# A relational graph layer on one core: loads in other pieces, bookkeeping moved between the table's steps, more gather buffers and a new written order

## The chip, the cores and the metric

The kernel runs on one core of a Trainium2 chip. The metric is the device time of one execution in microseconds (us), taken as the median of several runs. All data are float32 or int32 in DRAM; the inputs are laid out in other shapes on the host before the launch, and that takes no device time.

## The reference

One layer of a graph network with 625 nodes of width 512, 20,625 edges sorted by their target, and four relations:

```python
h = relu(layernorm(x))
for r in range(4):
    w_r = where(edge_type == r, edge_weight, 0)
    total_msg += (h[src] @ W_rel[r] + b_rel[r]) * w_r[:, None]
agg = segment_sum(total_msg, dst) / maximum(segment_sum(edge_weight, dst), 1)[:, None]
x1  = layer_norm(h + h @ W_self + b_self + agg, ln1_g, ln1_b)
ffn = gelu(x1 @ W_ffn1 + b_ffn1) @ W_ffn2 + b_ffn2          # 512 -> 1024 -> 512
out = x + layer_norm(x1 + ffn, ln2_g, ln2_b)
```

The edges are random, so the message rows have to be fetched by index or summed through a matrix that is built from the indices.

## The kernel before

**Tiles and blocks.** The nodes lie in five blocks of 128 (`NB`), the edges in 162 tiles of 128 (`NT`). As the edges are sorted by target, each tile belongs to one block or to two neighbours: tiles 0 to 30 to block 0, 130 to 161 to block 4, and the rest to blocks 1 to 3 and to the borders between blocks. Blocks 0 and 4 are called outer (`OUTER`), blocks 1 to 3 inner. A table of 4 x 5 = 20 chunks (`NC`) of 128 rows holds h @ W_rel[r] + b_rel[r] for every relation and node block.

**First stage: 20 steps.** The step number is r * NB + i. `table_rows` (L470) multiplies the transposed normalised x of block i with `wr_sb[r]`, four f32 matmuls; VectorE (DVE) scales the sum out of PSUM into `tr` (L483), adds the bias and has it stored to the table in DRAM; the last chunks stay in SBUF too (`kept`). Between these steps the rest of the bookkeeping is issued, each piece at a step that a constant names:

- Edge sums of the outer blocks. For block 0 and the first 15 tiles of block 4 (`LINES`), `line_columns` and `line_sums` work out for every edge the cell of a 128 x 2560 matrix that it adds to, joining the weights of equal cells, and GpSimd (POOL) scatters the weights to the cleared `cells` in DRAM with one indirect DMA a tile, 46 in all (`scatter`, L750; columns become ready at the steps of `COLUMNS_AT`, two scatters are issued in each of the steps 0 to 2 and all that are ready in later ones). The remaining 17 tiles of block 4 are "banked": they become one-hot matrices on DVE (`node_hots` L648, `weighted_hots` L666, the first of them at `HOTS_AT`) that are multiplied on TensorE (PE) in `outer_sum` (L680).
- `outer_columns` and `edge_columns` (at `COLUMNS_OF_EDGES_AT`) turn the loaded edge columns into float and into table rows `row_i`; `group_columns` and `degree_columns` follow at `GROUPS_AT`.
- `degree_hots` (L844, at `DEGREE_HOTS_AT` and, for the outer tiles, `OUTER_HOTS_AT`), `degree_sums` and `degree_end` (`DEGREES_AT`) make the sums of the edge weights and the counts of edges for each node; `spread_rows` (`SPREAD_AT`, L970 to L977) spreads them, `counts` among them, and `first_edges` (L906, `FIRST_AT`) multiplies the counts on PE to find where each node's edges begin. `load_first_edges` then has POOL gather `x_edges`, three indirect DMAs.
- The layer norm of x in other blocks: `centre_x` and `spread_x` on ScalarE (ACT), `rsqrt_pow` (L399) on POOL, at `NORM_AT` and `ROOT_AT`. Two norms are made ahead of the first step by `pre_norm`.
- `set_limits` (L534): 72 small ACT writes, half at step 4 and half at step 6 (`LIMITS_AT`), that `count_outside` (L542) uses to see whether an edge lies outside the range its tile was planned for. In that case a general loop runs at the end; with these inputs it doesn't.
- `tensor_add` of bias rows on x (L1235, `ADDS_AT`) and of the identity on `ws_sb` (L1245, `SELF_AT`).

**Loads.** They are issued by hand at the start, in this order: the two column halves of x block 0 (one on ACT's queue, one on that of SyncE, SP), quarters 0 and 1 of `wr_sb[0]`, x block 1, quarter 2, the line of edges of block 0 (`load_line`, 128 overlapping windows of one row), quarter 3, x block 2, bias rows, x blocks 3 and 4, the clearing of the cells, the edge columns, and later ones.

**Second stage.** It is a list of 700 operations (`Plan.op`), each with its engine, what it comes after and which buffers it takes and gives back. `Plan.written` issues them in the order that the constant `ORDER` writes out; all engines follow that one list, each its own part of it. If `ORDER` is empty, `Plan.times` makes an order from the costs; the constants `CELLS`, `FIRSTS`, `LAND` and `LATE` are read only there. The operations are:

- for the inner blocks and borders, in the order (3,4), (0,1), (1), (1,2), (2,3), (3), (2): POOL gathers table rows by `row_i` into one of ten buffers `ms` (L1312, 99 tiles, and three rows from `gather_first`). Three tiles make a group with common targets: ACT scales the first row (`first_row`), DVE adds the other two (`row_added`, L1348), then ACT and DVE split the sum into a high and a low fp32r part (`high`, `low`) and PE multiplies both with the one-hot `oh` (`edge_sum`, L1373), or, where the group stands whole (`parted`, `WHOLE`: every second group of the last sum, and its last three), one f32 product. In the last sum PE runs five small matmuls (`spin`, L1400) ahead of each of its last four (`SPINS`) units.
- for the outer blocks, 20 `chunk_sum` products each (L1489) of the matrix `sums_w`, loaded back from `cells`, with the table's chunks.
- for every block: `self_part` (L508), the first norm, `turn` and its copies (L1552), `ups` (L1058) with gelu, `downs` (L1078), the final norm (L1088 to L1103) and the stores. Block 2 comes last. Its final norm takes its root by `root_steps`: a square root on ACT, whose function table an extra `root_of` activation loads ahead, and a division step on DVE, for which `g2_bc` is scaled beforehand. The other blocks take their root by `rsqrt_steps` or, where `ROOTS` says POOL, by a power on POOL.

Of the kernel before, what the change touches and what calls it, by code (L numbers as in the profile page):

```python
# [16 lines left out]
P = 128  # L17
EG = 3
# [3 lines left out]
LINES = 999, 15  # L22


class EdgePlan:
# [84 lines left out]
class Plan:  # L110
# [48 lines left out]
    def times(self):  # L159
# [5 lines left out]
        while left:  # L165
# [27 lines left out]
            if not can:  # L193
                times = [e[0] for e in back] + list(free.values())
                times += [max(a.at + d for a, d in o.after) for o in left
                          if o.after and all(a.at is not None for a, _ in o.after)]
                t = min(x for x in times if x > t + 1e-6)
        return order


@with_exitstack
def gnn_layer(ctx, tc, x, edges, edge_line, edge_groups, w_self, w_rel, w_ffn1, w_ffn2, rows_in, bf_in, out, n_edges):

# [73 lines left out]
    def load_x(b0, b1):  # L277
        nc.sync.dma_start(xs[:, b0:b1, :], x[ep.first[b0]:ep.first[b0] + (b1 - b0) * P, :].rearrange("(b p) d -> p b d", p=P))
# [1490 lines left out]
```

## Time and profile before

| | |
|---|---|
| median of 3 runs | 258.41 us (257.94 to 258.63) |
| profiled execution | 257.69 us, span 255.8 us |
| mean granted TensorE clock | 0.992 |
| PE busy | 240.3 us, 94% of the span |
| DVE busy | 196.8 us, 77% |
| POOL busy | 171.5 us, 67% |
| ACT busy | 112.2 us, 44% |
| DMA | 59.44 MB, 232 GB/s over the span |

The span runs from the first to the last recorded instruction; the execution's time has what lies around it as well, here 1.9 us. In the lists of instructions a row gives the start, the length (us), the engine, the line of the program, the operation with output <- input, the shapes, how many instructions were joined, and in brackets how long the engine stood idle before it and what released it ("issue": nothing that the profile shows). A grouped row gives the count, the busy sum, the mean in ns, and the idle time before the group's instructions. A row of a window gives the span, then the busy time and the count for PE, PEld (weight loads of PE), DVE, ACT and POOL, then the granted clock, and the DMA engines' busy share and rate. Busy time of PE is the time that matmuls are in flight, so 94% is no statement on how much of it is needed.

### The profile page before, as it was taken

The page shows a single profiled execution, that of the slowest core. Times are in us where ns is not written, and L with a number is a line of the kernel's source. Part 1 is how long each engine was busy: PE and PEld are TensorE (multiplying, and loading weights), DVE is VectorE, ACT ScalarE, POOL GpSimd, SP SyncE. Part 2 cuts the span into 40 slices and gives each one's busy share as a digit, 9 for nine tenths or more (in the row PEclk, how much of TensorE's full clock was granted, in tenths as well). Part 3 has the DMA queues.
Part 4 walks back from the last instruction along what each step waited for, and adds up shares of the span by engine and source line. Part 5 has one row for each costly group of instructions (what it writes and reads, how often), then busy time and mean ns, then how long its engine had stood idle before and what let it go on. Part 6 is the DMA issues. An engine that isn't in the chain of part 4 may idle for free.

```text
span 255.8 us, 3608 instructions
## 1 busy us (share of the span) xinstructions
PE 240.3 (94%) x1051; PEld 141.9 (55%) x1051; DVE 196.8 (77%) x466; ACT 112.2 (44%) x345; POOL 171.5 (67%) x218
## 2 busy tenths in 40 slices
PE   7899999999969997997999999999999999978992
PEld 6354444444434753544545575666986668536871
DVE  3694699999996329997898889997795897767153
ACT  3378700000610007766147555747666565542620
POOL 5028888988998877877777777777777777701000
PEclk9999999999997999999999999999999999999999
DMA  6999999994361499887999986677777777621021
GB/s 175 345 406 409 377 350 349 331 324 167 83 249 41 110 342 281 302 279 241 304 324 361 376 300 196 188 214 197 214 215 209 204 190 192 214 65 41 3 82 43
DMA packets 23998, 59.44 MB, mean 232 GB/s; under 512 B 4420, under 2 KB 8744, under 8 KB 22823
## 3 DMA queue, kind: packets, MB, share of 16 engines
q0 software_dynamic: 9728, 26.79, 35.0%
q1 hardware_dynamic: 13920, 30.91, 33.7%
q10 hardware_dynamic: 326, 1.48, 1.9%
q8 instruction: 9, 0.15, 0.2%
q14 instruction: 15, 0.11, 0.2%
HBM read 49.99 MB, written 9.17 MB: 231 GB/s over the span
## 4 chain that ended last, share of the span: by engine, by line
PE 35%; DVE 31%; issue 12%; POOL 8%; DMA 8%; ACT 2%; SPq 1%; DVEq 0%; POOLq 0%; ACTq 0%
PE ps L1058 8%; PE acc L1489 7%; PE ps L1078 6%; PE acc L1373 5%; POOL ms L1312 4%; PE ps L508 4%; DVE tr L483 4%; PE ps L470 3%; DVE z L496 3%; POOL cells L750 3%; DMA line<-in_edge_line_dram 3%; DMA ms<-table,row_i 3%; DVE add L1348 3%; DMA x_edges<-in_edge_groups_dram,x_group 2%; DVE same L737 2%
## 5 line engine op out<-in xcount | busy, mean ns | idle before, releaser
L1312 POOL DMA_INDIRECT ms<-table,row_i x99 | 99.6, 1006 | 30.2 <-issue 14.8
L470 PE MATMUL ps<-wr,T 128*128 128x512 f32 (+2 forms) x168 | 72.6, 587 | 0.5 <-DMA wr<-in_L_gnn_W_rel_dram 0.5
L750 POOL DMA_INDIRECT cells<-weight,cell x46 | 52.8, 1148 | 15.5 <-DVE tr L483 8.2
L470 PEld LDWEIGHTS ps<-wr,T 128*128 128x128 f32 x168 | 31.3, 194 | 35.7 <-issue 31.9
L1348 DVE SCALAR_TENSOR_TENSOR add<-ms,wgt_g,add 128x512 f32<-128x512 f32 x55 | 40.5, 749 | 6.4 <-DMA ms<-table,row_i 3.5
L1058 PEld LDWEIGHTS ps<-T,w_sb 128*128 128x128 f32 x320 | 38.5, 192 | 5.4 <-issue 1.7
L1058 PE MATMUL ps<-T,w_sb 128*128 128x128 f32 (+2 forms) x320 | 39.4, 276 | 1.2 <-ACT T L1552 0.8
L1078 PE MATMUL ps<-w_sb,gT 128*128 128x512 f32 (+2 forms) x96 | 36.4, 522 | 0.0
L666 ACT ACTIVATE ohw<-os,w 128x128 fp32r<-128x128 f32 x34 | 10.8, 388 | 48.5 <-DVE os L648 48.5
L1318 ACT ACTIVATE add<-ms,wgt_g 128x512 f32<-128x512 f32 x30 | 20.4, 685 | 20.6 <-DVE el L1326 13.4
L1489 PE MATMUL acc<-tr,sums_w 128*128 128x512 f32 x60 | 29.3, 595 | 0.0
L1078 PEld LDWEIGHTS ps<-w_sb,gT 128*128 128x128 f32 x96 | 16.8, 191 | 13.9 <-issue 11.2
L1326 DVE TENSOR_TENSOR el<-add,eh 128x512 fp32r<-128x512 f32 x25 | 16.9, 685 | 6.1 <-PE acc L1373 3.7
L1322 ACT CAST eh<-add 128x512 fp32r<-128x512 f32 x25 | 14.6, 585 | 15.2 <-DVE add L1348 15.1
L1373 PE MATMUL acc<-eh,oh 128*128 128x512 f32 x34 | 18.0, 544 | 1.9 <-ACT eh L1336 1.4
L508 PE MATMUL ps<-ws_sb,T 128*128 128x512 f32 x40 | 18.7, 593 | 0.0
L1373 PE MATMUL acc<-el,oh 128*128 128x512 f32 x34 | 17.5, 538 | 0.2 <-DVE el L1340 0.2
L1064 ACT ACTIVATE gT<-ps,bf 128x128 f32<-128x128 f32 (+1 forms) x40 | 13.5, 359 | 7.0 <-PE ps L1058 6.7
L483 DVE SCALAR_TENSOR_TENSOR tr<-ps,rx,brel_bc 128x512 f32<-128x512 f32 x15 | 11.2, 745 | 5.6 <-POOL rx L399 5.6
L1489 PEld LDWEIGHTS acc<-tr,sums_w 128*128 128x128 f32 x60 | 10.6, 190 | 7.9 <-issue 6.0
L508 PEld LDWEIGHTS ps<-ws_sb,T 128*128 128x128 f32 x40 | 7.4, 190 | 7.1 <-issue 6.9
L1373 PEld LDWEIGHTS acc<-eh,oh 128*128 128x128 f32 x34 | 6.5, 190 | 7.4 <-issue 3.3
(240 smaller groups left out, 310.8 us busy)
## 6 DMA issues: line engine op xcount, KB each, us to landing
tr<-table SPq DMA_DIRECT2D x11, 512.0 KB, 5.5
w_sb<-in_L_gnn_W_ffn_dram SPq DMA_DIRECT2D x2, 2048.0 KB, 10.5
table<-tr SPq DMA_DIRECT2D x15, 256.0 KB, 5.9
wr<-in_L_gnn_W_rel_dram SPq DMA_DIRECT2D x3, 1024.0 KB, 7.6
cells<-zeros SPq DMA_DIRECT2D x2, 1280.0 KB, 9.2
ms<-table,row_i POOLq DMA_INDIRECT x99, 4.0
rows<-in_rows_dram SPq DMA_DIRECT2D x1, 1280.0 KB, 12.3
sums_w<-cells ACTq DMA_DIRECT2D x1, 1280.0 KB, 8.3
```

The source lines that it names most:

```text
L470: nc.tensor.matmul(p_[:, :h.stop - h.start], hT[i][:, k, :], wr_sb[r][:, k, h], start=(k == 0), stop=(k == KD - 1))
L483: made_row.append(nc.vector.scalar_tensor_tensor(m[:, h], p_[:, :h.stop - h.start], rx[:, i, 1:2], brel_bc[:, r * D + h.start:r * D + h.st ...
L508: nc.tensor.matmul(p[0], hT[i][:, k, :], ws_sb[:, k, :], start=(k == 0), stop=(k == KD - 1))
L750: s = nc.gpsimd.indirect_dma_start(out=cells[i][:, :], out_offset=bass.IndirectOffsetOnAxis(ap=cell[i][:, k:k + 1], axis=0), in_=weight[i] ...
L1058: nc.tensor.matmul(pu[:, low:nn + first], w1_sb[:, k, f * P:(f + 1) * P], x1T_b()[:, k, low:nn + first], start=(k == 0), stop=(k == KD - 1))
L1078: nc.tensor.matmul(po[h][:n, :w], box["gT"][:, f, at], w2_sb[:, f, c], start=(f == 0), stop=(f == KF - 1))
L1312: nc.gpsimd.indirect_dma_start(out=ms[j], out_offset=None, in_=table[:, :], in_offset=bass.IndirectOffsetOnAxis(ap=row_i[:, j:j + 1], axis=0))
L1318: nc.scalar.activation(box["sum"], ms[j], AF.Copy, scale=wgt_g[:, (j - GROUP0) // EG, 0:1])
L1326: nc.vector.tensor_sub(box["low"], box["sum"], box["high"].bitcast(F32))
L1348: nc.vector.scalar_tensor_tensor(to, ms[j], wgt_g[:, k, q:q + 1], box["sum"], op0=ALU.mult, op1=ALU.add)
L1373: nc.tensor.matmul(acc[bs], w.bitcast(F32) if of.dtype == F32 else w, of, start=first, stop=last)
L1489: nc.tensor.matmul(acc[b,], sums_w[b][:, c, :], kept[(b, c) if (b, c) in kept else c], start=first, stop=last)
```

## The change

- **Loads.** x comes in a second layout `x_by_row` (partition, block, column), in which one partition's rows are contiguous; x block 0 is loaded in two halves of the partitions, and its statistics are taken over the whole width at once (`x_stats`). `edge_line` is laid out with one contiguous row for each partition, and the line of block 0 comes in two pieces: three fields, and the weights later, after the bias rows. `wr_sb[0]` comes in two halves in place of four quarters, both ahead of the line.
- **Tiles.** 14 tiles of block 4 are scattered in place of 15, and 18 are banked. One scatter is issued in step 0, three in step 1, four in step 2.
- **Bookkeeping.** `set_limits` takes a slice: 18 of the writes for the lower limits come ahead of the first transposed copies, the rest after them, and the upper limits at step 4. `outer_columns` and `edge_columns` go from step 5 to 2, `group_columns` and `degree_columns` from 6 to 4, `degree_hots` from 9 and 12 to 5 and 6, those of the outer tiles from 15 and 16 to 6 and 8, `degree_end` from 14 to 9, `spread_rows` from 16 to 11, `first_edges` from 17 to 13; the third call of `next_columns` from step 4 to 3. The additions to x go from 15, 17, 18 to 5, 9, 16, the identity from 13 to 15, the pre-made one-hots from 13, 14, 16 to 14, 15, 16. The powers of blocks 3 and 4 are one instruction at step 2. The edge types in float (`typ_f`) have a tile of their own that ends with the first stage.
- **Gather buffers.** When `chunk_sum` has used them, the two `sums_w` matrices (five buffers each) and the five `kept` chunks are appended to `ms`: 25 buffers in place of 10, each given back to the order at the matmul that used it last.
- **Last rows.** `WHOLE` is 5. The last group of the last sum isn't joined: its three tiles are units of one tile each, whose one-hots carry the weights (`edge_hots`), and whose rows go from the gather straight into f32 products. `SPINS` is 6.
- **Roots.** `root_steps`, `root_of` and both scalings of `g2_bc` are gone; block 2's final root is taken by POOL.
- **Order.** `ORDER` is a new list, of 702 operations (PE 222 to 227, DVE 200 to 198, ACT 150 to 148, POOL 104 to 105, SP 19 and 19).

The diff, without the numbers of `ORDER` and without the places that pass `x_by_row` on:

```diff
-LINES = 999, 15
+LINES = 999, 14
...
 ORDER = [
...
 ]
...
     def load_x(b0, b1):
-        nc.sync.dma_start(xs[:, b0:b1, :], x[ep.first[b0]:ep.first[b0] + (b1 - b0) * P, :].rearrange("(b p) d -> p b d", p=P))
+        nc.sync.dma_start(xs[:, b0:b1, :], x_by_row[:, b0:b1, :])
...
-    def load_line(i):
-        at = sum(n * P + 2 * NEAR + 1 for _, _, n in lines[:i])
-        n = lines[i][2]
-        nc.sync.dma_start(line[i], bass.AP(tensor=edge_line.tensor, offset=edge_line.offset + at,
-                                           ap=[[n, P], [edge_line.shape[1], 4], [1, n + 2 * NEAR + 1]]))
+    def load_line(i, f0=0, f1=4):
+        at = sum(4 * (n + 2 * NEAR + 1) for _, _, n in lines[:i])
+        w = lines[i][2] + 2 * NEAR + 1
+        nc.sync.dma_start(line[i][:, f0:f1, :].rearrange("p f w -> p (f w)"), edge_line[:, at + f0 * w:at + f1 * w])
...
-    nc.scalar.dma_start(xs[:, 0, D // 2:], x[:P, D // 2:])
-    nc.sync.dma_start(xs[:, 0, :D // 2], x[:P, :D // 2])
-    load_wr(0, [(0, 1)])
-    load_wr(0, [(1, 2)])
+    nc.scalar.dma_start(xs[P // 2:, 0, :], x_by_row[P // 2:, 0, :])
+    nc.sync.dma_start(xs[:P // 2, 0, :], x_by_row[:P // 2, 0, :])
+    load_wr(0, [(0, 2)])
...
-    load_wr(0, [(2, 3)])
-    load_line(0)
-    load_wr(0, [(3, 4)])
+    load_wr(0, [(2, 4)])
+    load_line(0, 0, 3)
...
+    load_line(0, 3, 4)
...
     def x_stats(i):
-        st = work.tile([P, 2 if i == 0 else 1, 6], F32, tag="bn", name=f"st_x{i}", bufs=HOTS)
-        w = D // st.shape[1]
-        for h in range(st.shape[1]):
-            nc.vector.bn_stats(st[:, h, :], xs[:, i, h * w:(h + 1) * w])
+        st = work.tile([P, 6], F32, tag="bn", name=f"st_x{i}", bufs=HOTS)
+        nc.vector.bn_stats(st, xs[:, i, :])
...
-    fl = const.tile([P, 3, NT], F32, name="fl")
-    src_f, dst_f, typ_f = fl[:, 0, :], fl[:, 1, :], fl[:, 2, :]
+    fl = const.tile([P, 2, NT], F32, name="fl")
+    src_f, dst_f, typ_f = fl[:, 0, :], fl[:, 1, :], early.tile([P, NT], F32, name="typ_f")
...
-    def set_limits(a):
-        j0 = 0
-        for j in range(1, NT + 1):
-            if j == NT or limits[j][a] != limits[j0][a]:
-                nc.scalar.activation(lim[:, a, j0:j], node_row[:, :j - j0], AF.Copy, scale=0.0, bias=float(limits[j0][a]))
-                j0 = j
+    def set_limits(a, of=slice(None)):
+        at = [j for j in range(1, NT) if limits[j][a] != limits[j - 1][a]]
+        for j0, j in [*zip([0, *at], [*at, NT])][of]:
+            nc.scalar.activation(lim[:, a, j0:j], node_row[:, :j - j0], AF.Copy, scale=0.0, bias=float(limits[j0][a]))
...
-        nc.vector.tensor_copy(fl, ed[:, 0:3, :])
-        nc.vector.tensor_scalar(shift, fl[:, 0:2, :], float(ep.gap_at), float(ep.gap), op0=ALU.is_ge, op1=ALU.mult)
-        nc.vector.tensor_add(fl[:, 0:2, :], fl[:, 0:2, :], shift)
-        nc.vector.tensor_copy(node_i, fl[:, 0:2, :])
+        nc.vector.tensor_copy(fl, ed[:, 0:2, :])
+        nc.vector.tensor_copy(typ_f, ed[:, 2, :])
+        nc.vector.tensor_scalar(shift, fl, float(ep.gap_at), float(ep.gap), op0=ALU.is_ge, op1=ALU.mult)
+        nc.vector.tensor_add(fl, fl, shift)
+        nc.vector.tensor_copy(node_i, fl)
...
-    def root_steps(box, first):
-
-        def root():
-            nc.scalar.activation(box["t"][:, 1:2], box["t"][:, 0:1], AF.Sqrt)
-
-        def improve():
-            v, y, a = (box["t"][:, j:j + 1] for j in range(3))
-            nc.vector.reciprocal(y, y)
-            nc.vector.scalar_tensor_tensor(a, y, v, y, op0=ALU.mult, op1=ALU.mult)
-            nc.vector.scalar_tensor_tensor(y, a, 3.0, y, op0=ALU.subtract, op1=ALU.mult)
-
-        return [("root", "ACT", 0.25, root, [first]), ("r3", "DVE", 0.55, improve, ["root", "a"])]
-
     def feed_forward(x1T_b, box, members, name, halves=False, first=False, root="DVE", low=0):
...
-            norm += [] if halves else pow_step(got) if root == "POOL" else rsqrt_steps(got, "mean", root)
+            norm += pow_step(got) if root == "POOL" else rsqrt_steps(got, "mean", root)
...
-            norm += root_steps(got, "mean") if halves else []
...
-    SPINS = 4
+    SPINS = 6
...
-    HOTS_AT, SELF_AT, ADDS_AT = (13, 14, 16), 13, (15, 17, 18)
+    HOTS_AT, SELF_AT, ADDS_AT = (14, 15, 16), 15, (5, 9, 16)
...
-    WHOLE = 3
-    POW, ROOTS = 0.9, (("ACT", "ACT", "POOL", "ACT", "ACT"), ("ACT",) * 5)
-    CELLS, FIRSTS = 1.5, 5.0
+    WHOLE = 5
+    POW, ROOTS = 0.9, (("ACT", "ACT", "POOL", "ACT", "ACT"), ("ACT", "ACT", "POOL", "ACT", "ACT"))
+    CELLS, FIRSTS = 4.0, 0.5
...
-    COLUMNS_AT, LINE_AT, DEGREE_HOTS_AT = (0, 1, 4, 7, 10, 11, 13), 8, (9, 12)
-    COLUMNS_OF_EDGES_AT, GROUPS_AT, LOAD_AT, LIMITS_AT = 5, 6, 15, (4, 6)
-    DEGREES_AT, SPREAD_AT, FIRST_AT, OUTER_HOTS_AT = 14, 16, 17, (15, 16)
-    NORM_AT, ROOT_AT = ((0, 2), (1, 3), (2, 4)), ((1, 2), (2, 3), (3, 4))
+    COLUMNS_AT, LINE_AT, DEGREE_HOTS_AT = (0, 1, 3, 7, 10, 11, 13), 8, (5, 6)
+    COLUMNS_OF_EDGES_AT, GROUPS_AT, LOAD_AT, LIMIT_CUT, LIMITS_AT = 2, 4, 15, 18, 4
+    DEGREES_AT, SPREAD_AT, FIRST_AT, OUTER_HOTS_AT = 9, 11, 13, (6, 8)
+    NORM_AT, ROOT_AT = ((0, 2), (1, 3), (2, 4)), ((1, 2, 3), (2, 3, NB))
...
+        set_limits(0, slice(LIMIT_CUT))
...
+        set_limits(0, slice(LIMIT_CUT, None))
...
-                if step in dict(ROOT_AT):
-                    spread_x(dict(ROOT_AT)[step])
-                    rsqrt_pow(rx[:, dict(ROOT_AT)[step], :])
-                if step in LIMITS_AT:
-                    set_limits(LIMITS_AT.index(step))
+                for _, b0, b1 in (a for a in ROOT_AT if a[0] == step):
+                    for b in range(b0, b1):
+                        spread_x(b)
+                    nc.gpsimd.tensor_tensor(rx[:, b0:b1, 1], rx[:, b0:b1, 0], half.to_broadcast([P, b1 - b0]), op=ALU.pow)
...
-                for _ in range(2 if step < 3 else len(columns)):
+                if step == LIMITS_AT:
+                    set_limits(1)
+                for _ in range((1, 3, 4)[step] if step < 3 else len(columns)):
...
-                nc.vector.tensor_scalar(ohs[0][:, q, :], row, d[:, j_:j_ + 1], wgt[:, j_:j_ + 1],
+                to, w_ = j_, wgt[:, j_:j_ + 1]
+                if GROUP0 <= j_ < GROUP0 + EG * GROUPS:
+                    g_, q_ = divmod(j_ - GROUP0, EG)
+                    to, w_ = j_ - q_ + EG // 2, wgt_g[:, g_, q_:q_ + 1]
+                nc.vector.tensor_scalar(ohs[0][:, q, :], row, d[:, to:to + 1], w_,
...
-            if GROUP0 <= j < GROUP0 + EG * GROUPS and (j - GROUP0) % EG:
+            if GROUP0 <= j < GROUP0 + EG * GROUPS and (j - GROUP0) % EG and (bs != order_of[-1] or j + EG <= tiles[-1]):
...
+    more_rows = {}
+    for b in OUTER:
+        of = sums_w[b].rearrange("p c n -> p (c n)")
+        more_rows[b] = [len(own_buffers["ms"]) + i for i in range(NC * P // D)]
+        own_buffers["ms"] += [of[:, i * D:(i + 1) * D] for i in range(NC * P // D)]
+    for c in range(NL, NC):
+        more_rows[OUTER[1], c] = [len(own_buffers["ms"])]
+        own_buffers["ms"].append(kept[c])
...
-                  give=["tr"] if c < NL and (c + NL) % CH == CH - 1 else [], lag=0.25, rank=(2, 2 + 0.01 * i), level=1.5)
+                  give=(["tr"] if c < NL and (c + NL) % CH == CH - 1 else []) + [
+                      ("ms", n) for n in more_rows.get((b, c), []) + (more_rows[b] if last else [])],
+                  lag=0.25, rank=(2, 2 + 0.01 * i), level=1.5)
...
-    turned_g2, root_of = [], const.tile([P, 1], F32, name="root_of")
...
-        if last:
-            turned_g2 = [op("DVE", 0.4, lambda: nc.vector.tensor_scalar(g2_bc, g2_bc, -RS / 2, None, op0=ALU.mult),
-                            after=turned_g2),
-                         op("ACT", 1.5, lambda: nc.scalar.activation(root_of, ones, AF.Sqrt), after=gel)]
...
-                behind_ = turned_g2 if last and name == "mean" else []
+                behind_ = []
...
-            if not last:
-                turned_g2.append(made["a"])
...
-        nc.vector.tensor_scalar(g2_bc, g2_bc, -2 / RS, None, op0=ALU.mult)
...
-        edge_line.append(_np.stack([
+        near = _np.arange(P)[:, None] * n + _np.arange(n + 2 * NEAR + 1)
+        edge_line += [line[near] for line in (
...
-                (a["edge_weight"].view(_np.int32), _np.zeros(room, _np.int32)))]))
+                (a["edge_weight"].view(_np.int32), _np.zeros(room, _np.int32))))]
...
+    x_by_row = _np.ascontiguousarray(_np.stack([x[at:at + P] for at in ep.first], axis=1))
...
```

More of the change, by code (lines that the diff above doesn't have):

```diff
@@ L201, in gnn_layer @@
 @with_exitstack
-def gnn_layer(ctx, tc, x, edges, edge_line, edge_groups, w_self, w_rel, w_ffn1, w_ffn2, rows_in, bf_in, out, n_edges):
+def gnn_layer(ctx, tc, x, x_by_row, edges, edge_line, edge_groups, w_self, w_rel, w_ffn1, w_ffn2, rows_in, bf_in, out, n_edges):
     nc = tc.nc
@@ L1758 @@
     arrays, args = {}, []
-    for name, v in [("x", x), ("edges", edges), ("edge_line", edge_line), ("edge_groups", edge_groups), *((k, a[k]) for k in _WS), ("rows", rows), ("bf", bf)]:
+    for name, v in [("x", x), ("x_by_row", x_by_row), ("edges", edges), ("edge_line", edge_line), ("edge_groups", edge_groups), *((k, a[k]) for k in _WS), ("rows", rows), ("bf", bf)]:
         arrays[f"in_{name}_dram"] = v
```

60 rows, old and new, of the table ORDER are left out of this document.

## The prediction

> **What bounds the kernel now.** I read the page first, then GpSimd's timeline (POOL, the engine without a gap), then TensorE's (PE) at its few gaps, then the tail.
>
> ```profile
> PE 240.3 (94%) x1051; PEld 141.9 (55%) x1051; DVE 196.8 (77%) x466; ACT 112.2 (44%) x345; POOL 171.5 (67%) x218
> L1312 POOL DMA_INDIRECT ms<-table,row_i x99 | 99.6, 1006 | 30.2 <-issue 14.8
> L750 POOL DMA_INDIRECT cells<-weight,cell x46 | 52.8, 1148 | 15.5 <-DVE tr L483 8.2
> 17.42 1.71 POOL L750 DMA_INDIRECT cells<-weight,cell  x1 [8.21 <-DVE tr L483]
> 20.70 0.59 POOL L399 TENSOR_TENSOR rx<-rx,half 128x1 f32<-128x1 f32 x1
> 68.88 4.04 POOL L750 DMA_INDIRECT cells<-weight,cell  x1 [0.17 <-issue]
> 73.22 2.18 POOL L750 DMA_INDIRECT cells<-weight,cell  x1 [0.17 <-issue]
> 82.06 0.96 POOL L750 DMA_INDIRECT cells<-weight,cell  x1 [0.17 <-issue]
> 83.32 1.04 POOL L750 DMA_INDIRECT cells<-weight,cell  x1 [0.17 <-issue]
> 89.77 0.95 POOL L1312 DMA_INDIRECT ms<-table,row_i  x1 [0.19 <-issue]
> 91.03 0.96 POOL L1312 DMA_INDIRECT ms<-table,row_i  x1 [0.30 <-issue]
> 221.80 1.33 POOL L1312 DMA_INDIRECT ms<-table,row_i  x1 [0.30 <-issue]
> ```
>
> From 17.42 to 223.13 POOL is one unbroken string: 46 scatters at a pitch of 1.27 us (82.06 to 83.32), three `x_edges` gathers, 102 row gathers at 1.26 (89.77 to 91.03). Idle time before a gather is the constant 0.30 whatever is named as releaser, so POOL waits for no buffer today. From the last gather to the end are 33 us. PE has nearly no room either; its gaps:
>
> ```profile
> 10.57 1.99 PE L470 MATMUL ps<-wr,T 128*128 128x512 f32 x4 [0.48 <-DMA wr<-in_L_gnn_W_rel_dram]
> 75.62 0.39 PE L906 MATMUL ps<-counts,before 128*128 128x3 f32 x2 [2.10 <-DVE counts L975]
> 78.67 0.34 PEld L470 LDWEIGHTS ps<-wr,T 128*128 128x128 f32 x1 [0.52 <-issue]
> 79.52 0.34 PEld L470 LDWEIGHTS ps<-wr,T 128*128 128x128 f32 x1 [0.52 <-issue]
> 72.50 0.19 PEld L470 LDWEIGHTS ps<-wr,T 128*128 128x128 f32 x1 [0.24 <-issue]
> 78.00:80.00 2.00, 2.00 (x4) 0.83 (x3) 1.93 (x7) 0.00 (x0) 1.67 (x4) 0.50 0.35 121
> 80.00:82.00 2.00, 2.00 (x5) 0.74 (x4) 0.15 (x1) 0.00 (x0) 1.73 (x4) 0.75 0.01 0
> 85.36 0.58 PE L680 MATMUL ps<-od,ohw 128*128 128x440 f32 x2
> 86.00:132.00 46.00, 42.59 (x211) 23.20 (x210) 35.08 (x97) 22.64 (x50) 35.65 (x36) 1.00 0.87 286
> 132.00:225.60 93.60, 93.19 (x441) 61.73 (x440) 79.71 (x140) 56.63 (x151) 69.81 (x71) 1.00 0.77 233
> 227.06 1.13 PE L1373 MATMUL acc<-ms,oh 128*128 128x512 f32 x2 [1.44 <-DVE ms L1348]
> ```
>
> The windows give span, then busy time of PE, PEld, DVE, ACT, POOL, then granted clock. PE fills the table until 85.4 with one stall of 2.10, behind which the clock reads 0.50. In the gather stage it idles 3.41 us before 132, 0.41 up to 225.60, and 1.44 for the last rows. So PE and POOL are both on the path, within about 2 us of each other.
>
> **The change, part by part.** The profiled execution took 257.69 us (span 255.8); the median is 258.41, 0.72 above. Sums are made against the first; the forecast is put on the median.
>
> *PE, table stage.* The stall at 75.62 is `first_edges` waiting for `counts`, which stood on DVE behind two 1.56 us one-hot blocks. `SPREAD_AT` goes from step 16 to 11, `FIRST_AT` from 17 to 13: two steps of slack in place of one, some 3.5 us more. I take the 2.10 as gone. What is late next is DVE's emptying of `ps`; its moved work (`outer_columns` to step 2, the columns to step 4) fills idle DVE time:
>
> ```profile
> 20.00:30.00 10.00, 10.00 (x27) 4.58 (x26) 4.33 (x6) 9.20 (x79) 8.91 (x16) 1.00 1.04 398
> 30.00:40.00 10.00, 10.00 (x25) 4.48 (x24) 9.30 (x40) 0.09 (x1) 8.88 (x16) 1.00 1.00 347
> 23.07 7.01 ACT L534 ACTIVATE lim<-node_row 128x35 f32<-128x35 f32 x72
> 11.21 0.60 ACT L430 ACTIVATE junk<-xs 128x512 f32<-128x512 f32 x1 [1.36 <-DMA xs<-in_x_dram]
> ```
>
> DVE has 5.67 us free in 20 to 30. The 72 limit writes cost ACT 0.097 each: 18 before the first copies (1.75) and some 18 after fit ACT's waits for x there; the rest stays near 27 us. Both cost nothing; without that cover at most 1.75 would fall on the first copies. With the stall goes the half clock: weight loads stand 0.85 apart (78.67 to 79.52) instead of 0.43 (72.50: 0.24 + 0.19), which over the two windows loses 2 x 0.5 + 2 x 0.25 = 1.5 us. [...]
>
> Loads: x and `wr_sb[0]` in fewer, longer pieces, the last quarter of `wr_sb[0]` now ahead of `line[0]`. PE waited until 10.57 for that quarter; the line ahead of it is 128 x 4 x 158 x 4 B = 0.32 MB, 0.8 us at the 398 GB/s of the row from 20 to 30, so the bounds are 0 and 0.8. Then x block 2 (ACT at 11.21) binds, and it still comes behind most of the line, so I take 0.3. The second piece of the line (its weights) is one more issue on SP, against one fewer for `wr_sb[0]`. Table stage on PE: 2.1 + 1.5 + 0.3 = 3.9 earlier.
>
> *POOL, table stage.* One scatter less (46 to 45): 1.27. The three later `rsqrt_pow` become two: 0.59 and the 0.17 behind it, 0.76. The first scatter waits for the cleared cells or for its weights, whose line is issued one place earlier; which of the two comes last isn't shown, so I bound it by 0 and the same 0.8 and take 0.4, the middle. Together 2.4: gathers from 87.4. The last table store, 3.9 earlier by PE, is in by then. The `x_edges` gathers pass nothing on POOL: the last scatters are issued in step 13 too, ahead of them. What hides their landing is the gathers of the first two sums, which need none of it. Against it: the long scatters stand under DVE blocks with two SBUF inputs.
>
> ```profile
> 68.71 1.56 DVE L844 TENSOR_TENSOR sums_w<-rel,row_w 128x1368 bf16<-128x1368 bf16 x1
> 70.20 1.28 DVE L1235 TENSOR_TENSOR xs<-xs,rows 128x512 f32<-128x512 f32 x2
> 71.40 0.68 DVE L1245 TENSOR_TENSOR rows<-rows,bf_bc 128x512 f32<-128x512 f32 x1
> 77.00 1.31 DVE L1235 TENSOR_TENSOR xs<-xs,rows 128x512 f32<-128x512 f32 x2
> ```
>
> The scatter at 68.88 ends 0.9 us after L1245 does, as if it began only there; the two cost 4.04 + 2.18 - 2 x 0.96 = 4.3. The change spreads these blocks (`OUTER_HOTS_AT` to steps 6 and 8, `ADDS_AT` to 5, 9, 16), all still beside scatters; a scatter that starts just ahead isn't held (the pair at 77.00). I take the same 4.3, bounds 0 and 8.6.
>
> *Gather stage.* 15 more gather buffers free nothing by themselves: POOL had no wait to lose. The new order lets PE and DVE lag further behind the gathers (up to 16 rows outstanding, from 10). PE gets two more f32 products, one more banked tile and, ahead of the last product, two spins:
>
> ```profile
> 222.89 2.74 PE L1373 MATMUL acc<-ms,oh 128*128 128x512 f32 x6
> L680 PE MATMUL ps<-od,ohw x34: 228/282/773, 85.4 to 124.4; 128*128 128x260 f32 x7, 128*128 128x280 f32 x5, 128*128 128x240 f32 x4, 128*128 128x220 f32 x3
> 226.26 0.75 DVE L1348 SCALAR_TENSOR_TENSOR ms<-ms,wgt_g,add 128x512 f32<-128x512 f32 x1 [1.10 <-DMA ms<-table,row_i]
> 231.46 0.71 PE L1400 MATMUL spin<-zeros 128*128 128x256 bf16 x5
> ```
>
> 2 x 0.91 + 2 x 0.28 + 2 x 0.71 = 3.8. The spins cost nothing where PE waits anyway (bounds 0 and 1.4; I take all of it, since PE has no gap there today). DVE loses two row adds (1.5) and gains three weighted one-hots, ready ahead of their rows; it has 13.9 us free in the window to 225.6, so the extra tile's one-hots cost nothing either. PE line: its backlog ended at 225.62; -3.9 + 3.8 - 1.9 (half of the 3.82 idle, between none and all of it) = 223.6, and the last product 1.1: 224.7, from 228.19. POOL line: the last row lands at 226.26 - 2.4 = 223.9, the add of 0.75 is gone, the product ends at 225.0. The later one holds: 3.2 earlier.
>
> *Tail.*
>
> ```profile
> 233.49 0.65 ACT L1552 COPY T<-ps 128x256 f32<-128x256 f32 x2 [6.29 <-DVE ow L1088]
> 232.81 0.64 ACTq L1131 DMA_DIRECT2D out_dram<-ow  x1
> 230.20 1.00 POOL L399 TENSOR_TENSOR rs_z<-rs_z,half 128x1 f32<-128x1 f32 x1 [7.07 <-DVE rs_z L389]
> 249.21 0.15 DVE L391 TENSOR_SCALAR rs_y<-mv_y 128x1 f32<-128x1 f32 x1
> 250.58 0.88 DVE L1103 SCALAR_TENSOR_TENSOR ow<-ow,rs_y,xs 128x320 f32<-128x320 f32 x2
> ```
>
> ACT's last copies wait behind a store that ACT's own queue issues at 232.81; the new order puts that store among the last activations. But PE now has two down parts and a spin (4.3 us) ahead of the turn: copies at about 4.9 after the last product, from 5.3: 0.4. The final root goes from ACT and DVE (249.36 to 250.58, 1.22) to POOL's power (0.09 + 1.00 + 0.04): 0.1. The square root's table load and the scaling of `g2_bc` go too; both ran beside the last matmuls and cost nothing.
>
> Sum: 3.2 + 0.4 + 0.1 = 3.7; 257.69 becomes 254.0, and the median **254.7**.
>
> **Rivals.** (1) The DVE blocks hit the scatters harder: from 2.4 us more on, the gathers start at 89.8 as before, only the dropped add and the tail (1.25) are left: 257.2. For it: 68.88; against: the shorter blocks. [...] (2) Slower: the stall moves instead of going. DVE is 9.3 busy of 10 from 30 us on; if `counts` or a `ps` copy at steps 11 to 15 is again 2 us late, the half clock comes with it, PE keeps only 0.3, and its 3.8 more land on the end: -0.3 + 3.8 - 1.4 (the wait for the last rows) - 0.5 (tail) = 1.6 later, 260.0. It decides once PE gains less than 1.9 in the table stage and wins nothing of its other idle time. (3) More: the first scatter and half of the 4.3 at their good ends (0.4 + 2.1) and the other half of PE's idle gone (1.9): PE then ends its products 1.9 earlier still, at 222.8, and rules: 252.5. (4) The change does not do what it says: buffers and order move nothing, gains and 3.8 cancel, 258.4.
>
> **How the numbers follow.** Forecast 0.55 (own range 253.2 to 256.4), (1) 0.16, (2) 0.12, (3) 0.09, (4) 0.08. A measurement of this kernel tells about 0.3% (0.8 us). Range 252.2 to 258.4: it holds (1), (3) and (4), leaves out (2) and some of (3). Faster 0.77 (forecast, (3) and most of (1)), same 0.10, slower 0.13.
>
> **What would show it.** No PE stall and no clock under 1 between 70 and 85, table end near 81; 45 scatters, first gather near 87.4, last one near 219.4; products of single rows as the last L1373; no ACT square root. Wrong if PE stalls over 1.5 us before 81, if scatters of over 2 us add to more than 8, or if PE falls behind the gathers by more than 2 us at the end.

## The result, and the profile after

Over 20 executions of each kernel the median went from 257.19 to 254.44 us, 2.75 less; the ratio is 0.9895 with a 95% interval of 0.9866 to 0.9924. The profiled execution took 253.69 us (span 251.9), 4.0 less than that of before: of this pair, the one of before lies 0.5 above its median and the one of after 0.75 below. Six of the runs below took 301 to 319 us, and the kernel before beside them 296 to 304, because PE, DVE and ACT stood still together (in `rows_joined` for 9.0 us at a time, from 202.48 to 211.49); of those only the stretch ahead of the first such pause is read.

The page of the changed kernel, its parts 1 and 4:

```profile
PE 241.4 (96%) x1067; PEld 143.8 (57%) x1067; DVE 194.6 (77%) x464; ACT 111.7 (44%) x345; POOL 164.5 (65%) x216
PE 61%; issue 11%; DVE 11%; DMA 10%; POOL 3%; ACT 1%; SPq 0%; DVEq 0%; POOLq 0%; ACTq 0%
```

PE's share of the chain that ended last is 61% now. PE's timeline and the windows, first of before at the start (the row from 8 to 12 and the transposes of the third block), then of after:

```profile
8.00:12.00 4.00, 2.94 (x10) 1.40 (x11) 2.50 (x9) 1.34 (x4) 0.56 (x1) 1.00 1.02 362
13.25 0.60 PE L406 MATMUL ps<-ident,z 128*128 128x128 f32 x4
```

```profile
7.53 3.10 PE L466 MATMUL ps<-wr,T 128*128 128x512 f32 x4 [1.26 <-DMA wr<-in_L_gnn_W_rel_dram]
8.00:12.00 4.00, 4.00 (x10) 2.05 (x9) 3.28 (x10) 0.85 (x5) 0.80 (x1) 0.57 0.99 366
14.88 0.60 PE L404 MATMUL ps<-ident,z 128*128 128x128 f32 x4
62.28 20.88 PE L466 MATMUL ps<-wr,T 128*128 128x512 f32 x56
78.00:86.00 8.00, 8.00 (x95) 5.39 (x95) 3.56 (x6) 0.57 (x1) 5.11 (x8) 1.00 0.31 97
86.00:132.00 46.00, 44.86 (x153) 23.77 (x152) 37.68 (x100) 26.74 (x63) 33.36 (x34) 1.00 0.86 291
132.00:225.60 93.60, 92.05 (x446) 61.59 (x445) 76.89 (x141) 53.67 (x140) 66.58 (x69) 1.00 0.75 231
```

The stall for `counts` and the half clock at 78 to 82 are gone: the last 56 matmuls of the table run through to 83.16. But PE starts worse. It waits 1.26 us for the first half of `wr_sb[0]`, and the clock from 8 to 12 reads 0.57, so the same transposes come at 14.88 in place of 13.25. Of 3.8 gained (2.10 and 1.7), 1.6 were spent at the start; the table ends 2.45 earlier (85.61 to 83.16), and what gave the remaining 0.3 isn't traced. In the gather stage PE idles 1.14 us before 132 and 1.55 from there to 225.60, together 2.69 where it was 3.82.

POOL, and DVE where they meet:

```profile
17.76 1.20 POOL L745 DMA_INDIRECT cells<-weight,cell  x1 [7.31 <-DMA cells<-zeros]
50.32 1.57 DVE L839 TENSOR_TENSOR sums_w<-rel,row_w 128x1368 bf16<-128x1368 bf16 x1
50.76 1.98 POOL L745 DMA_INDIRECT cells<-weight,cell  x1 [0.17 <-issue]
79.17 0.96 POOL L745 DMA_INDIRECT cells<-weight,cell  x1 [0.17 <-issue]
86.01 0.95 POOL L1296 DMA_INDIRECT ms<-table,row_i  x1 [1.96 <-ACT ow L882]
99.00 0.55 DVE L618 TENSOR_TENSOR sum<-ps,sums_w 128x220 f32<-128x220 f32 x1 [4.62 <-DMA sums_w<-cells]
100.48 0.94 POOL L1296 DMA_INDIRECT ms<-table,row_i  x1 [2.15 <-DVE outer_deg L890]
102.45 1.21 POOL L1296 DMA_INDIRECT ms<-table,row_i  x1 [1.03 <-DVE el L1324]
218.34 0.95 POOL L1296 DMA_INDIRECT ms<-table,row_i  x1 [0.30 <-DVE el L1310]
```

The scatters end at 80.13 in place of 85.63, and one of them takes about 2 us or more where two did. POOL has slack for the first time: 1.96 us before the first gather, then 2.15 and 1.03 for buffers, behind a DVE that stood 4.62 us for the load of the second cell matrix. These are the ten old buffers: ten rows are gathered from 86.01 on, the eleventh waits until 100.48, and the first row in a new buffer (`sums_w`) is gathered at 123.86. The last gather is issued 3.46 earlier (221.80 to 218.34).

The last rows and the tail:

```profile
223.68 1.88 PE L1361 MATMUL acc<-ms,oh 128*128 128x512 f32 x4
229.80 0.65 ACT L1550 COPY T<-ps 128x256 f32<-128x256 f32 x2 [10.06 <-PE ps L404]
245.79 0.99 POOL L397 TENSOR_TENSOR rs_y<-rs_y,half 128x1 f32<-128x1 f32 x1 [17.21 <-DVE rs_y L387]
```

The last product ends at 225.56, 2.63 earlier, and PE waits for no row there.

### The profile page after: what moved, and what is told of

Read it like the earlier page. It is cut to its first block, busy times and chain, and to the rows that moved or that the text cites. A ratio compares the mean times of both kernels' runs of the same rounds, so it can differ in the third digit from the quotient of the medians.

```text
span 251.9 us, 3638 instructions
## 1 busy us (share of the span) xinstructions
PE 241.4 (96%) x1067; PEld 143.8 (57%) x1067; DVE 194.6 (77%) x464; ACT 111.7 (44%) x345; POOL 164.5 (65%) x216
## 4 chain that ended last, share of the span: by engine, by line
PE 61%; issue 11%; DVE 11%; DMA 10%; POOL 3%; ACT 1%; SPq 0%; DVEq 0%; POOLq 0%; ACTq 0%
PE ps L466 28%; PE ps L1040 10%; PE ps L1060 10%; PE acc L1361 6%; DMA sums_w<-cells 4%; PE acc L1477 3%; DVE add L1332 3%; DVE z L492 3%; DMA ms<-table,row_i 3%; DMA wr<-in_L_gnn_W_rel_dram 2%; POOL ms L1296 2%; DVE el L1324 2%; DMA sums_w<-table,row_i 1%; PE ps L404 1%; PE ps L877 1%
## 5 line engine op out<-in xcount | busy, mean ns | idle before, releaser
L1296 POOL DMA_INDIRECT ms<-table,row_i x60 | 59.6, 993 | 22.5 <-issue 7.6
L745 POOL DMA_INDIRECT cells<-weight,cell x45 | 47.6, 1058 | 14.4 <-DMA cells<-zeros 7.3
L1296 POOL DMA_INDIRECT sums_w<-table,row_i x29 | 27.9, 964 | 8.8 <-issue 4.0
L1477 PE MATMUL acc<-tr,sums_w 128*128 128x512 f32 x60 | 30.0, 595 | 0.1
L661 ACT ACTIVATE ohw<-os,w 128x128 fp32r<-128x128 f32 x36 | 11.5, 389 | 30.2 <-DVE os L643 27.5
L1332 DVE SCALAR_TENSOR_TENSOR add<-ms,wgt_g,add 128x512 f32<-128x512 f32 x30 | 22.3, 749 | 1.9 <-ACT add L1302 1.6
L1361 PE MATMUL acc<-eh,oh 128*128 128x512 f32 x34 | 16.9, 529 | 0.9 <-DVE z L492 0.9
L1332 DVE SCALAR_TENSOR_TENSOR add<-sums_w,wgt_g,add 128x512 f32<-128x512 f32 x18 | 13.5, 750 | 1.1 <-ACT add L1302 0.9
L1302 ACT ACTIVATE add<-ms,wgt_g 128x512 f32<-128x512 f32 x16 | 10.9, 687 | 7.3 <-DVE el L1310 4.1
L492 DVE SCALAR_TENSOR_TENSOR z<-acc,rdeg,z 64x512 f32<-64x512 f32 (+1 forms) x10 | 7.5, 748 | 8.1 <-PE acc L1361 6.2
```

What stands on the lines that cost most here:

```text
L492: nc.vector.scalar_tensor_tensor(z[at, b, :], of[at, :], scale[at, :], z[at, b, :] if k else bself_bc[at, :], op0=ALU.mult, op1=ALU.add)
L745: s = nc.gpsimd.indirect_dma_start(out=cells[i][:, :], out_offset=bass.IndirectOffsetOnAxis(ap=cell[i][:, k:k + 1], axis=0), in_=weight[i] ...
L1296: nc.gpsimd.indirect_dma_start(out=ms[j], out_offset=None, in_=table[:, :], in_offset=bass.IndirectOffsetOnAxis(ap=row_i[:, j:j + 1], axis=0))
L1332: nc.vector.scalar_tensor_tensor(to, ms[j], wgt_g[:, k, q:q + 1], box["sum"], op0=ALU.mult, op1=ALU.add)
L1361: nc.tensor.matmul(acc[bs], w.bitcast(F32) if of.dtype == F32 else w, of, start=first, stop=last)
L1477: nc.tensor.matmul(acc[b,], sums_w[b][:, c, :], kept[(b, c) if (b, c) in kept else c], start=first, stop=last)
```

## The experiments

Theory A: PE sets the end, and the moved bookkeeping frees it. Rivals: B, the landing of the last rows sets it; C, the new order and buffers carry the gain. D and E/F concern the clock and the long scatters. Each time below stands beside the kernel before on the same chip. The first four runs have six executions each, beside eleven of the kernel before (median 257.62 us); their intervals are 1.8 to 2.3 us wide.

**The old loads in the new kernel.** `loads_back`:

```diff
-    load_wr(0, [(0, 2)])
+    load_wr(0, [(0, 1)])
+    load_wr(0, [(1, 2)])
...
-    load_line(0, 0, 3)
+    load_line(0)
+    load_wr(0, [(3, 4)])
```

> The changed kernel with its first loads in the old pieces and the old order (x block 0 in two column halves with split statistics, four quarters of wr_sb[0], the line of edges in one piece ahead of the last quarter, from the new layouts). Theory A (PE sets the end, and the new pieces cost it the 1.26 us wait at 7.5 and the clock of 0.57 from 8 to 12): the second step's transposes start near 13.3 in place of 14.88, the clock reads 1.0 from 8 to 12, the table ends near 81.5 in place of 83.1, the last row product 1.6 us earlier, the execution about 1.6 us shorter than the changed kernel (252.1 profiled, 4 to 5.5 us below the kernel before). Theory B (the landing of the last gathered rows sets the end): the table ends earlier too, but the end moves by less than 0.5 us.

Measured: 253.61 us, ratio 0.9834 (0.9798 to 0.9869). PE's timeline of this run:

```profile
12.58 0.64 PE L405 MATMUL ps<-ident,z 128*128 128x128 f32 x4
59.75 0.38 PE L904 MATMUL ps<-counts,before 128*128 128x3 f32 x2 [0.60 <-DVE counts L973]
77.70 4.06 PE L469 MATMUL ps<-wr,T 128*128 128x512 f32 x17
228.58 0.61 PE L405 MATMUL ps<-ident,z 128*128 128x128 f32 x4
```

The third block's transposes come 2.30 earlier than in the changed kernel; a wait of 0.60 for `counts` appears, since PE is now ahead of DVE; the table ends 1.40 earlier. At the last turn (228.58 against 229.38) 0.80 is left. So in this pair of profiles the loads make 2.3 us at the start and a third of that at the end: between A's 1.6 and B's 0.5. By the medians the run is 4.0 us below the kernel before, where the change had 2.75.

Most of the 2.3 isn't the pieces themselves. The run `steps_back` (below) keeps the new loads, and PE waits there too, yet at full clock:

```profile
7.22 1.95 PE L466 MATMUL ps<-wr,T 128*128 128x512 f32 x4 [1.08 <-DMA wr<-in_L_gnn_W_rel_dram]
8.00:12.00 4.00, 3.88 (x13) 1.70 (x12) 3.28 (x12) 2.17 (x8) 0.55 (x1) 1.00 1.02 333
13.23 0.60 PE L404 MATMUL ps<-ident,z 128*128 128x128 f32 x4
```

Its third block comes at 13.23, 0.65 later than with the old loads and 1.65 earlier than in the profile of the changed kernel. The half clock at the start came in that profile (0.57) and, by the same four matmuls, which took 3.27 there in place of 1.95, in the one of `no_lead_spins`, but not in every execution: 8 of the 20 of the changed kernel had a mean granted clock of 0.999 or 1.0, which leaves no room for it (0.43 x 4 us lost are 0.7% of the span). Their median is 254.44 us, that of the others without the slowest (256.65) 254.17: no cost of the half clock at the start is seen in the time.

**Two spins fewer.** `no_lead_spins` returns from the first two calls of `spin`:

> The changed kernel without the first two of the small spin products, those that its order puts among the last row products. Theory A (PE is the line that sets the end): last row product 0.9 us earlier (0.43 to 0.47 of issue for each), end 0.9 us earlier. Theory B (the rows' landing sets it): nothing, PE waits for rows instead.

Measured: 252.42 us, ratio 0.9783 (0.9738 to 0.9828), the fastest of all. PE:

```profile
222.85 1.88 PE L1362 MATMUL acc<-ms,oh 128*128 128x512 f32 x4
228.55 0.61 PE L404 MATMUL ps<-ident,z 128*128 128x128 f32 x4
```

The last product ends at 224.73, 0.83 earlier, without a wait, though the table ended 0.3 later in this run. A holds at the end of this profile: PE's queue, not the rows, was last. By the medians the run is 5.2 us below the kernel before, 2.4 more than the change; the spins account for 0.83 of that, and the rest isn't explained.

**The bookkeeping put back, and moved alone.** `steps_back` sets the constants of the changed kernel to the old steps; `steps_only` sets those of the kernel before to the new ones (with the limits' writes, which the edge columns read):

```diff
-    DEGREES_AT, SPREAD_AT, FIRST_AT, OUTER_HOTS_AT = 9, 11, 13, (6, 8)
+    DEGREES_AT, SPREAD_AT, FIRST_AT, OUTER_HOTS_AT = 14, 16, 17, (15, 16)
...
```

> The changed kernel with the constants of the bookkeeping put back to the steps of before (one-hots, identity, additions, degree sums, counts, first edges, edge columns); loads, buffers, order and last rows stay as changed. Theory A (the moved bookkeeping carries the gain): PE stalls 2 us again near 75 with a clock of 0.5 behind it, scatters of 4 and 2 us come back, the table ends 3 to 4 us later (86 to 87), and the time is that of the kernel before within 1 us. Theory C (the gather stage's order and buffers carry it): the time stays 2 us or more below the kernel before.

> The kernel before with only the bookkeeping moved to the new steps (the limits' writes move with it, since the edge columns read them); old loads, 15 scattered tiles, old order, ten gather buffers, old last rows and root. Theory A: no stall near 75 and no clock under 1, no scatter over 2.2 us, table end near 81.7 (3.6 earlier), gathers from about 86, and the time 2.5 to 3.5 us below the kernel before, as much as the whole change or nearly. Theory C: less than 1 us, since the old order and its ten buffers hold the gather stage where it was.

Measured: `steps_back` 255.24 us, ratio 0.9892 (0.9855 to 0.9930); `steps_only` 255.18 us, 0.9898 (0.9855 to 0.9941). Each has about as much as the whole change (2.4 us each, against 2.75). PE, windows, POOL and DVE of `steps_back`:

```profile
68.05 3.65 POOL L745 DMA_INDIRECT cells<-weight,cell  x1 [0.16 <-issue]
72.00 2.18 POOL L745 DMA_INDIRECT cells<-weight,cell  x1 [0.17 <-issue]
74.69 0.39 PE L901 MATMUL ps<-counts,before 128*128 128x3 f32 x2 [1.20 <-DVE counts L970]
75.82 8.85 PE L466 MATMUL ps<-wr,T 128*128 128x512 f32 x24
76.00:78.00 2.00, 2.00 (x4) 0.81 (x4) 1.97 (x7) 0.00 (x0) 1.83 (x4) 0.78 0.36 132
78.00:80.00 2.00, 2.00 (x4) 0.84 (x3) 0.92 (x2) 0.00 (x0) 1.68 (x4) 0.50 0.02 1
80.00:82.00 2.00, 2.00 (x6) 0.93 (x5) 0.76 (x2) 0.00 (x0) 1.78 (x4) 0.87 0.01 0
88.80 0.95 POOL L1296 DMA_INDIRECT ms<-table,row_i  x1 [0.19 <-issue]
99.43 0.53 DVE L618 TENSOR_TENSOR sum<-ps,sums_w 128x220 f32<-128x220 f32 x1 [3.50 <-DMA sums_w<-cells]
218.93 0.94 POOL L1296 DMA_INDIRECT ms<-table,row_i  x1 [0.30 <-DVE el L1310]
```

Stall, half clock and long scatters are all back, as A said; the table ends at 84.67, 1.51 later than in the changed kernel (though its start was 1.65 earlier, so that the steps themselves cost 3.2), and the gathers start 2.79 later. Yet DVE, held by the load of the cells, goes on at 99.43 against 99.00, and the last gather stands at 218.93 against 218.34. The changed kernel spends its head start between 86 and 103, on DVE's 4.62 and POOL's 3.18 of waiting, and A's time falls: the last rows of `steps_back` come only 0.6 later, its end 0.5. The load itself, in the changed kernel and in `steps_back`:

```profile
89.78 0.32 SPq L764 DMA_DIRECT2D sums_w<-cells  x1
91.28 0.32 SPq L764 DMA_DIRECT2D sums_w<-cells  x1
```

It is issued 1.50 earlier, as much as PE is ahead, and takes 9.2 us to land in place of 8.1. In the new order SP issues it behind a load of a table chunk, which goes out at 88.70, when PE's product of 87.65 has ended; the old order issued it ahead of those (at 88.09 before the change, where DVE didn't wait for it, and at 85.09 in `steps_only`). No run here moves that one load. PE and POOL of `steps_only`:

```profile
60.59 0.38 PE L904 MATMUL ps<-counts,before 128*128 128x3 f32 x2 [1.28 <-DVE counts L973]
60.00:62.00 2.00, 1.41 (x11) 1.37 (x12) 1.84 (x17) 0.00 (x0) 1.67 (x5) 1.00 0.12 38
62.00:64.00 2.00, 2.00 (x6) 0.81 (x6) 1.97 (x3) 0.00 (x0) 1.83 (x3) 1.00 0.61 206
86.79 0.95 POOL L1312 DMA_INDIRECT ms<-table,row_i  x1 [0.19 <-issue]
224.50 1.12 PE L1373 MATMUL acc<-ms,oh 128*128 128x512 f32 x2 [0.93 <-DVE ms L1348]
```

Under the old order the gathers start 2.98 earlier than before and the last product comes 2.56 earlier (227.06 to 224.50), behind the last addition: there the rows do set the end. The wait for `counts` moved, to 60.59, rather than went (1.28), and the clock stayed at 1.00. So C is right of the first run and A nearly of the second (2.4 for its 2.5 to 3.5), neither of the whole: each part alone brings about the gain, and the two don't add. Which of the loads, the order, the buffers, the last rows and the root gives the gain of `steps_back` isn't separated.

**The half clock.** `before_filled_2` is the kernel before with 14 small matmuls on PE ahead of the product that waits for `counts`:

```diff
                 if step == FIRST_AT:
+                    for _ in range(14):
+                        nc.tensor.matmul(fill[:, :176], zeros[:, :P], zeros[:, :176], start=True, stop=True)
                     first_edges()
```

> The same kernel as before_filled, whose run fell on a chip where DVE, ACT and PE stood still together for 14 us in the table stage, so that the wait in question didn't arise. As there: theory A (the half clock follows from PE standing idle): the wait for the counts is still there but filled, clock 1.0 from 76 to 82, table end 1.5 to 1.7 us earlier than 85.4. Theory D: clock 0.5 behind it again, table end near 85.4.

Measured: 259.10 us, beside 258.99 for the kernel before on that chip, one execution each. PE and POOL:

```profile
75.78 0.38 PE L906 MATMUL ps<-counts,before 128*128 128x3 f32 x2 [0.59 <-DVE counts L975]
76.91 7.15 PE L470 MATMUL ps<-wr,T 128*128 128x512 f32 x24
90.21 0.95 POOL L1315 DMA_INDIRECT ms<-table,row_i  x1 [0.19 <-issue]
```

The product comes when it did, but the 24 matmuls behind it take 7.15 in place of 8.85: the half clock had cost 1.70 on top of the wait, and with less idling it didn't come. That speaks against D, in one execution: a wait doesn't always bring it, as 1.28 at a clock of 1.00 in `steps_only` shows. The table ends at 84.06, and the time doesn't move, for POOL starts where it did. The same filling at the start of the changed kernel, `warm_start`:

> The changed kernel with PE kept busy in its first two waits: five more warming matmuls ahead of the first transposes and eight behind them. Theory A: clock 1.0 from 8 to 12 in place of 0.57, second transposes near 9 to 9.3 in place of 10.43, table end near 81.6 in place of 83.1, and the execution 0.5 to 1.7 us shorter than the changed kernel, as far as the gather stage passes the gain on. Theory D: the clock stays at 0.57 there.

This run met the pauses from 46 us on (314.56 us, before 302.59); ahead of them:

```profile
7.77 1.95 PE L466 MATMUL ps<-wr,T 128*128 128x512 f32 x4 [0.95 <-DMA wr<-in_L_gnn_W_rel_dram]
8.00:12.00 4.00, 3.93 (x12) 1.68 (x12) 3.07 (x9) 1.76 (x9) 0.78 (x1) 1.00 1.03 346
13.72 0.60 PE L404 MATMUL ps<-ident,z 128*128 128x128 f32 x4
```

The weights landed 0.24 later, and the third block is 1.16 earlier all the same, at full clock. So some 1.2 to 1.4 of the 1.6 lost at the start were the clock, not the wait itself. That the filling kept the clock up isn't shown: `steps_back` kept it without, behind a wait of 1.08.

**The long scatters.** `before_one_input_2` is the kernel before with the additions of L1235 and L1245 as one-input operations, so that it leaves the bias rows out of its result:

```diff
-                        nc.vector.tensor_add(xs[:, b, :], xs[:, b, :], b2_bc)
+                        nc.vector.tensor_scalar(xs[:, b, :], xs[:, b, :], 1.0, None, op0=ALU.mult)
```

> The same kernel as before_one_input (additions at L1235 and L1245 replaced by one-input operations on the same tiles; the bias rows are left out of the sums), which ran on the same other chip. Theory E (two-input operations on SBUF hold the issue): the scatter that takes 4.04 at 68.88 takes 2.0 to 2.4 here, the one under the second one-hot block stays near 2.2, POOL ends its scatters some 1.7 us earlier. Theory F (any busy DVE or the load of the DMA engines): it stays near 4.

Measured: 255.34 us in one execution beside one of 258.99 of before. DVE and POOL:

```profile
69.09 3.24 POOL L750 DMA_INDIRECT cells<-weight,cell  x1 [0.17 <-issue]
70.41 0.74 DVE L1235 TENSOR_SCALAR xs<-xs 128x512 f32<-128x512 f32 x2
71.08 0.41 DVE L1245 TENSOR_SCALAR rows<-rows 128x512 f32<-128x512 f32 x1
72.64 2.18 POOL L750 DMA_INDIRECT cells<-weight,cell  x1 [0.17 <-issue]
```

Both E (2.0 to 2.4) and F (4) miss with 3.24. The scatter ends at 72.33, 0.84 behind L1245; before, it ended at 72.92, 0.84 behind L1245 too (72.08); in the changed kernel the one at 50.76 ends 0.85 behind L839. So the scatter beside these one-input operations, 0.37 each at L1235 in place of 0.64, was long as well: L1245 ended 2.40 behind the scatter's start in place of 3.20, and the scatter took 0.80 less. The place and the price of E stand by these figures; its condition was too narrow, for two inputs weren't needed here. The 3.65 us between the two executions are more than the scatter's 0.8 and aren't explained.

**Both improvements together, and the last rows joined again.** These runs met the pauses:

> The same kernel as old_loads_no_spins, whose run fell on the chip with the pauses: the changed kernel with its loads in the old pieces and order, without the two spin products among the last rows, and with the first edges' product at step 14. Theory A (PE sets the end, the gains of the two runs add): table end near 81.2, last row product done near 223.9, the execution 1.5 to 2 us below the changed kernel and 5 to 6 us below the kernel before. Theory B (the rows become the bound once PE gains): last product not before 224.3, with PE waiting for rows ahead of it.

> As old_loads_no_spins_2, but with the last three rows joined as before the change (first row scaled by ACT, two added by DVE, one f32 product in place of three; the order's list has the three operations at the places of the removed products, and no spins among the last rows). Theory A (PE sets the end, so two more f32 products of 0.86 us cost what they take until the rows' landing rules): the joined product ends 0.5 to 1.2 us earlier than in old_loads_no_spins_2, now behind the last addition, and the execution is that much shorter. Theory B (the rows' landing rules, for which the change was built): 0.75 us or more later, since the last addition stands between the landing and the product.

`old_loads_no_spins_2` took 306.19 us and `rows_joined` 305.56, beside 297.18 for the kernel before (ratios 1.0198 and 1.0177); before_filled, before_one_input and old_loads_no_spins had ended like that on another chip (305.65, 303.52 and 313.26; before 302.59). Pauses of all three engines, which no line of the kernel names, say nothing on A or B. Under them the four variants of the changed kernel came out 1.8 to 3.8% slower than the kernel before; why isn't shown. Whether the two improvements add, and whether the three last products pay, stays open.

## Why the prediction was right, and where it wasn't

- *Forecast.* 254.7 against 254.44, but from a base of 258.41 that 20 runs put at 257.19: the change forecast was 3.7, the medians moved 2.75 (2.0 to 3.4 by the interval), so the size was forecast about 0.9 too large. That 254.7 lies so near is luck: the base was 1.2 too high. The profiled pair, 4.0, flatters the size.
- *Stall and half clock.* Right, with 2.10 and 1.70 for 2.10 and 1.5. Rival (2), the stall that moves, came true elsewhere, in the profile: a wait of 1.26 at the start, with the half clock behind it, and the table ended at 83.16, not near 81.
- *Loads.* This step failed: 0.3 earlier was forecast, 1.6 later came. I priced the line that was moved behind the weights, and not that PE's first matmul needs only a quarter and now waits for half of `wr_sb[0]`: 0.95 to 1.68 in the four profiles with the new loads. How late that makes PE was chance: 1.6 with the half clock behind it, nothing against the kernel before (13.23 for 13.25) without, in `steps_back`. `loads_back` has neither.
- *POOL.* Forecast 2.4, measured 3.76 at the first gather and 5.5 at the last scatter. The term of the long scatters was mis-sized: their excess fell from 4.3 to 1.0 (1.98 less 0.96), while the first scatter came 0.34 later, held by the clearing of the cells. Rival (1) looked in the right place, for the 1.98 at 50.76 stands beside L839, but had its sign wrong.
- *Gather stage.* The forecast end was 225.0, from the rows; PE set it, at 225.56, with the spins and products that the prediction had added to it. Its line was forecast at 224.7: the table's end came 1.45 less early than the 3.9 in that sum, and PE's idle time fell by 1.1 where 1.9 was taken; against that, the added work came to some 2.4 by the same sum, not 3.8. Rival (4) and the forecast both missed why earlier gathers are worth little: DVE waits for the load of the cells until 99, and the ten old buffers are full by then, before a new one is used.
- *Tail.* 1.06 where 0.4 was forecast: the copies start 4.24 behind the last product in place of 5.30. The root gave 0.12 for 0.1.

## What to carry to other kernels

Ask of every earlier start which load or which engine will hold it next; here a head start of 2.8 us on one engine shrank to 0.6 behind one load that went out only 1.5 earlier and landed only 0.4 earlier. Work that fills time on a waiting engine, as the spins did, has to be taken out when that engine becomes the bound: two of them cost 0.8 us here. And measure parts alone and together, for two changes that remove the same slack look good one by one.

## What the runs showed of the hardware

The granted clock fell behind some single waits of PE and not behind others. Behind a wait of 1.26 us in the changed kernel it read 0.57 from 8 to 12, behind 2.10 in the kernel before 0.50 from 78 to 80 and 0.75 from 80 to 82, and behind 1.20 in `steps_back` 0.78, 0.50 and 0.87 in the three windows from 76 to 82. If the clock was 0.50 for as long as it was low, the first and the last of these give an estimated 3.4 us each: (1 - 0.57) x 4 / 0.5 and (0.22 + 0.50 + 0.13) x 2 / 0.5. Behind waits of 1.28 in `steps_only` and, at the start, of 1.08 in `steps_back` it read 1.00. What decides between waits of like length isn't shown.

Three long scatters of POOL ended 0.84 to 0.85 us behind the last of a row of DVE operations on SBUF that ran beside them: at 72.92 after 72.08 in the kernel before, at 72.33 after 71.49 in `before_one_input_2`, and at 52.74 after 51.89 in the changed kernel. They took 4.04, 3.24 and 1.98 us, where the scatter at 79.17 in the changed kernel took 0.96. The last operation was L1245 with two inputs, L1245 with one, and L839, with two inputs and alone.
